# Last phase of a convolution, attention and experts kernel: W inverse evicted by two engines for two images, six of the last image's tile pairs added by VectorE

## The chip, the cores and the metric

The kernel runs on one core of a Trainium2 chip, in float32. A core has five engines that run side by side, each with its own queue of instructions in a fixed order: TensorE (PE; matmuls and transposes, into the PSUM memory; its weight loads are listed apart as PEld), VectorE (DVE), ScalarE (ACT), GpSimd (POOL) and SyncE (SP; here it issues DMA transfers). An instruction that needs another engine's result waits on a semaphore, and everything behind it in its queue waits too. PSUM is where TensorE writes; VectorE and ScalarE read it and "evict" results into the larger SBUF memory. The metric is the device time of one execution in microseconds (us), lower is better.

## The reference, cut to what matters

The input x is 32 images of 128 channels and 64 x 64 pixels.

```python
# layer 0: x + K-operator convolution of the group-normalized x
x_f = tensor_product(xc, _c(k11), _c(k12), False)        # butterflies along H and W
w_f = tensor_product(wc, _c(kd1), _c(kd2), False) * math.sqrt(H * W)
prod = jnp.einsum('bihw,oihw->bohw', x_f, w_f)
out = tensor_product(prod, _c(k21), _c(k22), True)       # inverse along H and W
x = x + jnp.real(out)
# layer 1, per image: 4096 tokens of 128 channels
t = t + _L1_attn_ref(_ln_t(t), Wk, bk, Wv, bv)           # scores over channels, softmax
t = t + _L1_ffn_ref(_ln_t(t), router_w, router_b, expert_w, expert_b)
# experts: softmax over 8, the best two, weights made to sum to 1
top_p, top_i = jax.lax.top_k(router_probs, K)
expert_out = jnp.einsum('bnd,edc->bnec', x, expert_w) + expert_b
return jnp.einsum('bnk,bnkc->bnc', top_p, gathered)
```

The second half of it, the inverse transforms, attention and experts, is the phase that is changed. The kernel computes all eight experts for every token and sums them with weights ("gates") of which six of eight are zero.

## The kernel before

It has three phases. The first (to about 974 us) normalizes and transforms the images and stores the result to HBM; the second (to about 2732 us) mixes channels at every frequency and stores the products, pf; the third works image by image on pf and x and writes the output. Only the third is changed.

**An image in the last phase.** Four builders add its steps to a plan.

- `transfers(b)`: SyncE loads eight tiles r0 to r7 of pf (ten buffers) and the image itself, y (two buffers).
- `conv(b)`: for each r tile e, `w_inverse` has TensorE make a PSUM tile pu of 128 x 1024 (eight matmuls, L818; step "w"), in the pool cv with ONE buffer of two banks; `w_out` copies it into the SBUF tile u by ScalarE (L828; steps "wo", two per tile, one for each half oh of pu's partitions, with two copies of 64 x 512 each, r = 0 and 1, which go to partitions 0 to 63 and 64 to 127 of u). When all eight are in u, `h_inverse` makes four PSUM tiles py, in the same pool cv (L840; "h"), and `h_out` adds each to y on VectorE (L848; "ho").
- `front(b)`: transposes of y into token tiles (pt, L899), their copies into tk on ScalarE ("to", L904), statistics on VectorE ("sa", L873; "va", L881 to L886), a power on GpSimd ("pwa", L891), "na" on VectorE (L928), normalized tokens xg on ScalarE (L939), the Gram matrix pg (L950), the chain of the softmax (gs, pa, rows, pb, t1, sm, pr, pc, prx: small steps that go back and forth between TensorE, VectorE and ScalarE), the product pp with the tokens (L1038), scaled by ScalarE (L1051, L1055) and added to tk by VectorE (L1066), a second power ("pwb"), and the router: logits, two maxima, an exponent on ScalarE ("f5", L1132), and the gates ("gt", L1137 to L1141, result oh).
- `experts(b)`: 32 tiles of 128 tokens. For a group of four: normalized tokens xn (ScalarE, L1166), transposed px (L1176), xT. For each token tile i and half (four experts): `expert` makes PSUM tile pe of 128 x 512 (L1189, three buffers); `gated` multiplies it by the gates into tm on VectorE (step "m", L1200). For each PAIR of token tiles (i // 2, 16 pairs an image) `summed` adds the eight products and the token tile tk on GpSimd (step "s", five instructions: two of L1211, one of L1212, two of L1214). tm holds a pair and has two buffers. `back` transposes four token tiles (po, L1221), `store` copies them (so, L1227) and SyncE writes them out.

**The order.** A builder gives each step an engine, an estimated time, a due time (in slots of 114 us per image, with a shift for each kind), what it comes after, and which buffers it takes and frees. `Plan.run` walks a model of the five engines with these estimates and writes down the order in which each engine's steps start: the earliest due among those that are ready. That is the order of each queue in the built program. The steps of three images are in flight at once: conv of image b beside front of b - 1 and experts of b - 2. In the built program the waits are set by a framework, from the data and the buffers that the instructions touch; the steps' own "after" lists only set the order.

```python
    plan = Plan({"cv": 1, "pe": 3, "tl": 3, "r": 10, "x": 2, "xg": NG, "xn": 2, "xT": 2, "tm": 2, "so": 2, "gate": 2})
    SLOT = 114.0
```

The first images have nothing beside them, so at the beginning conv(0) stands alone, and conv(1) is beside front(0); at the end the experts of image 31 stand alone.

Of the kernel before, what the change touches and what calls it, by code (L numbers as in the profile page):

```python
# [90 lines left out]
def kernel(  # L91
# [720 lines left out]
    def conv(b):  # L812
        def w_inverse(e):

            def run():
                ps = tile_of["cv", b, e] = cps.tile([P, 8, P], F32, tag="cv", name=f"pu{b}_{e}")
                for k in range(8):
                    nc.tensor.matmul(  # L818
                        ps[:, k, :], rs[b, e][:, k * P : (k + 1) * P], qw.rearrange("w r m -> w (r m)"),
                        start=True, stop=True,  # L820
                    )
            return run

        def w_out(e, oh):
            def run():
                ps = tile_of["cv", b, e]
                for r in range(2):
                    nc.scalar.copy(  # L828
                        u[r * n : (r + 1) * n, :, oh * n + 8 * e : oh * n + 8 * e + 8],
                        ps[oh * n : (oh + 1) * n, :, r * n : (r + 1) * n].rearrange("h o w -> h w o"),  # L830
                    )
            return run

        def h_inverse(g):
            def run():
                ps = tile_of["cy", b, g] = cps.tile([P, 16 * n], F32, tag="cv", name=f"py{b}_{g}")
                for k in range(16):
                    for oh in range(2):
                        rows = slice(oh * n, (oh + 1) * n)
                        nc.tensor.matmul(  # L840
                            ps[rows, k * n : (k + 1) * n], u[:, 16 * g + k, rows], hm, start=True, stop=True
                        )
            return run

        def h_out(g):
            def run():
                acc = xs[b][:, :, 16 * g : 16 * g + 16]
                nc.vector.tensor_tensor(  # L848
                    acc, tile_of.pop(("cy", b, g)).rearrange("o (w h) -> o h w", h=n), acc, ALU.add
                )  # L850
            return run

        for e in range(8):
            at = b + 0.08 * e
            add(b, f"w{e}", "PE", 1.8, at, w_inverse(e), [f"r{e}"] + [(b - 1, f"h{k}") for k in range(4)], ("cv",), ("r",))
            for oh in range(2):
                add(
                    b, f"wo{e}_{oh}", "ACT", 1.2, at, w_out(e, oh),
                    [f"w{e}"] + [(b - 1, f"h{k}") for k in range(4)], (), ("cv",) if oh else (),
                )  # L860
        for g in range(4):
            at = b + 0.68 + 0.07 * g
            add(b, f"h{g}", "PE", 2.15, at, h_inverse(g), [f"wo{e}_{oh}" for e in range(8) for oh in range(2)], ("cv",))
            add(b, f"ho{g}", "DVE", 1.25, at, h_out(g), [f"h{g}", "x"], (), ("cv",))
# [292 lines left out]
    def experts(b):  # L1157
        t = tk[b % 2]

        def normal(g):  # L1160
            def run():
                rstd, nmr = tile_of["norm", b]
                x = tile_of["xn", b, g] = wp.tile([P, 4, P], F32, tag="xn", name=f"xn{b}_{g}")
                for k in range(4):
                    i = 4 * g + k
                    nc.scalar.activation(  # L1166
                        x[:, k, :], t[:, i, :], AF.Identity, bias=nmr[:, i : i + 1], scale=rstd[:, i : i + 1]
                    )
            return run

        def turn(g):
            def run():
                x = tile_of.pop(("xn", b, g))
                ps = tile_of["px", b, g] = tps.tile([P, 512], F32, tag="tl", name=f"px{b}_{g}")
                for k in range(4):
                    nc.tensor.transpose(ps[:, k * P : (k + 1) * P], x[:, k, :], ident)  # L1176
            return run

        def turned(g):
            def run():  # L1180
                x = tile_of["xT", b, g] = wp.tile([P, 4, P], F32, tag="xT", name=f"xT{b}_{g}")
                nc.scalar.copy(x.rearrange("p k c -> p (k c)"), tile_of.pop(("px", b, g)))
            return run

        def expert(i, half):
            def run():
                es = slice(4 * half, 4 * half + 4)
                ps = tile_of["pe", b, i, half] = eps.tile([P, 512], F32, tag="pe", name=f"pe{b}_{i}_{half}")
                nc.tensor.matmul(  # L1189
                    ps, tile_of["xT", b, i // 4][:, i % 4, :], ew_sb[:, es, :].rearrange("d e c -> d (e c)"),  # L1190
                    start=True, stop=True,
                )
            return run

        def gated(i, half):
            def run():
                es = slice(4 * half, 4 * half + 4)
                if i % 2 == 0 and half == 0:
                    tile_of["tm", b, i // 2] = wp.tile([P, 2, NE, P], F32, tag="tm", name=f"tm{b}_{i}")
                nc.vector.tensor_tensor(  # L1200
                    tile_of["tm", b, i // 2][:, i % 2, es, :],
                    tile_of.pop(("pe", b, i, half)).rearrange("p (e c) -> p e c", c=P),
                    tile_of["gate", b][:, i, es].unsqueeze(2).to_broadcast([P, 4, P]), ALU.mult,
                )
            return run

        def summed(j):
            def run():
                tm, lo = tile_of.pop(("tm", b, j)), 2 * j
                for k in range(2):  # L1210
                    nc.gpsimd.tensor_tensor(tm[:, k, 0:4, :], tm[:, k, 0:4, :], tm[:, k, 4:8, :], ALU.add)  # L1211
                nc.gpsimd.tensor_tensor(tm[:, :, 0:2, :], tm[:, :, 0:2, :], tm[:, :, 2:4, :], ALU.add)  # L1212
                for m in range(2):
                    nc.gpsimd.tensor_tensor(t[:, lo : lo + 2, :], t[:, lo : lo + 2, :], tm[:, :, m, :], ALU.add)  # L1214
            return run

        def back(g):
            def run():
                ps = tile_of["po", b, g] = tps.tile([P, 512], F32, tag="tl", name=f"po{b}_{g}")
                for k in range(4):  # L1220
                    nc.tensor.transpose(ps[:, k * P : (k + 1) * P], t[:, 4 * g + k, :], ident)  # L1221
            return run

        def store(g):
            def run():
                so = wp.tile([P, 512], F32, tag="so", name=f"so{b}_{g}")
                nc.scalar.copy(so, tile_of.pop(("po", b, g)))  # L1227
                nc.sync.dma_start(ov[b][:, g * 512 : (g + 1) * 512], so)
            return run

        s2 = b + 2
        for g in range(8):
            at = s2 + 0.125 * g
            add(b, f"xn{g}", "ACT", 1.7, at - 0.1, normal(g), ["nb"], ("xn",))
            add(b, f"px{g}", "PE", 0.55, at - 0.05, turn(g), [f"xn{g}"], ("tl", "xT"), ("xn",))
            add(b, f"xT{g}", "ACT", 0.6, at - 0.05, turned(g), [f"px{g}"], (), ("tl",))
            for k in range(4):
                i = 4 * g + k
                for half in range(2):
                    add(  # L1240
                        b, f"pe{i}_{half}", "PE", 0.86, at + 0.125 * (2 * k + half) / 8, expert(i, half), [f"xT{g}"],
                        ("pe",), ("xT",) if k == 3 and half else (),
                    )
                    add(
                        b, f"m{i}_{half}", "DVE", 0.7, at + 0.125 * (2 * k + half) / 8, gated(i, half),
                        [f"pe{i}_{half}", "gt"] + ([f"m{i - k % 2}_0"] if k % 2 or half else []), ("tm",) if k % 2 == 0 and half == 0 else (),
                        ("pe",) + (("gate",) if i == NT - 1 and half else ()),
                    )
                if k % 2:
                    add(  # L1250
                        b, f"s{i // 2}", "POOL", 5.45, at + 0.125 * (2 * k + 2) / 8, summed(i // 2),
                        [f"m{i - 1 + a}_{h}" for a in range(2) for h in range(2)], (), ("tm",),
                    )
            add(b, f"st{g}", "PE", 0.55, at + 0.25, back(g), [f"s{2 * g}", f"s{2 * g + 1}"], ("tl",))
            add(b, f"so{g}", "ACT", 0.6, at + 0.25, store(g), [f"st{g}"], (), ("tl",))
# [61 lines left out]
```

## Time and profile before

| | us |
|---|---|
| median of five runs (lowest, highest) | 6379.27 (6372.46, 6384.12) |
| the profiled execution | 6376.22 |
| its span, first to last instruction | 6374.5 |
| TensorE busy | 6118.0 (96%) |
| VectorE busy | 4196.8 (66%) |
| ScalarE busy | 3759.9 (59%) |
| GpSimd busy | 4204.5 (66%) |
| experts' matmuls, L1189 (4096 instructions) | 1985.7 |
| gated products, L1200 (2048) | 1353.0, 0.684 each |
| W inverse copies, L828 (1024) | 594.1, 0.580 each |
| GpSimd sums, L1211, L1212, L1214 | 1308.2, 652.8, 760.0 |

The profile comes from one execution. In its groups a row gives line, engine, operation, output <- input, shapes and count, then the busy time in us and the mean of one in ns, then the idle time of that engine before them and what ended it. In a timeline a row gives start and length in us, engine, line and operation, how many instructions were merged, and in brackets the idle time before and its releaser. A float32 matmul or transpose counts as two instructions on TensorE. The span in 40 slices, TensorE's busy tenths, the clock granted to it, and GpSimd:

```
PE   7999999999999999969999999999999999999987
POOL 2110005666666666506888888888888888888889
PEclk9999999999999999989999999999999999999999
```

The last phase begins in slice 18.

### The profile page before, as it was taken

What the parts mean: (1) busy time and instruction counts of PE and PEld (TensorE: products, weight loads), DVE (VectorE), ACT (ScalarE), POOL (GpSimd) and SP (SyncE); (2) the same over time, 40 slices, a digit from 0 to 9 for tenths busy, and PEclk for the clock granted to TensorE, in tenths of its full rate; (3) what the DMA queues carried; (4) which work ended last, traced back from release to release, by engine and by line L of the source; (5) the groups of instructions that cost most, each with busy time, mean ns of one, the idle gap of its engine ahead of it and who ended that gap; (6) DMA issues with size and microseconds to landing.
All of it is one profiled execution on the core that took longest, in us unless ns stands there. A gap on an engine that the chain in (4) does not pass through costs nothing. (4 is left out here: it accounts for less than half of the span.)

```text
span 6374.5 us, 218347 instructions
## 1 busy us (share of the span) xinstructions
PE 6118.0 (96%) x94922; PEld 4789.6 (75%) x94922; DVE 4196.8 (66%) x7626; ACT 3759.9 (59%) x7089; POOL 4204.5 (66%) x3780
## 2 busy tenths in 40 slices
PE   7999999999999999969999999999999999999987
PEld 7899998999999999966666666666666666666653
DVE  5555544555555555527787878777787878787776
ACT  6666663444444444446666667666667666666752
POOL 2110005666666666506888888888888888888889
PEclk9999999999999999989999999999999999999999
DMA  5666656666666666552121212222222212121100
GB/s 202 217 208 226 221 204 173 159 157 162 159 158 158 156 157 158 134 141 93 63 96 62 95 62 93 67 85 73 83 77 70 88 63 95 61 96 62 67 19 25
DMA packets 556965, 756.55 MB, mean 119 GB/s; under 512 B 58466, under 2 KB 321892, under 8 KB 551908
## 3 DMA queue, kind: packets, MB, share of 16 engines
q1 hardware_dynamic: 554096, 741.38, 38.4%
q8 instruction: 745, 12.21, 0.8%
q14 instruction: 216, 1.77, 0.1%
q10 hardware_dynamic: 1908, 1.19, 0.1%
HBM read 406.80 MB, written 335.54 MB: 116 GB/s over the span
## 5 line engine op out<-in xcount | busy, mean ns | idle before, releaser
L1189 PE MATMUL pe<-ew_sb,xT 128*128 128x512 f32 x4096 | 1985.7, 602 | 51.0 <-DVE tm L1200 50.7
L1200 DVE TENSOR_TENSOR tm<-pe,oh 128x512 f32<-128x512 f32 x2048 | 1353.0, 684 | 564.3 <-PE pe L1189 421.8
L1211 POOL TENSOR_TENSOR tm<-tm 128x512 f32<-128x512 f32 x1024 | 1308.2, 1293 | 307.8 <-DVE tm L1200 256.0
L1189 PEld LDWEIGHTS pe<-ew_sb,xT 128*128 128x128 f32 x4096 | 691.4, 191 | 523.7 <-issue 332.0
L623 PE MATMUL m<-f,s 128*64 128x64 f32 x32768 | 1068.7, 224 | 5.8 <-POOL s L574 4.4
L623 PEld LDWEIGHTS m<-f,s 128*64 128x64 f32 x32768 | 998.3, 138 | 67.4 <-POOL s L574 4.7
L574 POOL COPY s<-l 128x512 f32<-128x512 f32 x512 | 548.2, 1105 | 734.5 <-issue 654.4
L612 ACT COPY f<-g 128x1024 f32<-128x1024 f32 x512 | 518.7, 1013 | 671.1 <-PE g L601 644.2
L612 DVE COPY f<-g 128x1024 f32<-128x1024 f32 x512 | 627.0, 1225 | 348.0 <-PE g L601 340.1
L1214 POOL TENSOR_TENSOR tk<-tk,tm 128x256 f32<-128x256 f32 x1024 | 760.0, 742 | 80.3
L828 ACT COPY u<-pu 64x512 f32<-64x512 f32 x1024 | 594.1, 580 | 306.4 <-PE pu L818 295.4
L601 PE MATMUL g<-c,wst 9*128 9x128 f32 x16384 | 726.2, 287 | 25.7 <-ACT f L612 3.5
L1212 POOL TENSOR_TENSOR tm<-tm 128x512 f32<-128x512 f32 x512 | 652.8, 1275 | 40.1
L601 PEld LDWEIGHTS g<-c,wst 9*128 9x128 f32 x16384 | 579.8, 186 | 109.9 <-DVE f L612 69.4
L818 PEld LDWEIGHTS pu<-qw,r 128*128 128x128 f32 x4096 | 501.9, 196 | 169.4 <-ACT u L828 92.1
L633 DVE COPY o<-m 64x1024 f32<-64x1024 f32 x256 | 314.0, 1227 | 469.0 <-ACT o L633 421.5
L818 PE MATMUL pu<-qw,r 128*128 128x128 f32 x4096 | 520.8, 282 | 62.8 <-ACT u L828 52.9
L345 POOL TENSOR_TENSOR grstd<-gms,mhalf 128x1 f32<-128x1 f32 x32 | 17.7, 554 | 784.4 <-DVE gms L341 755.2
L414 PE MATMUL pf<-ph,v 128*128 128x128 f32 x4096 | 495.6, 279 | 19.3 <-issue 12.8
L576 POOL TENSOR_SCALAR s<-l 128x512 f32<-128x512 f32 x256 | 503.7, 1968 | 0.0
L414 PEld LDWEIGHTS pf<-ph,v 128*128 128x128 f32 x4096 | 470.2, 193 | 30.9 <-issue 14.4
L1227 ACT COPY so<-po 128x512 f32<-128x512 f32 x256 | 150.9, 590 | 574.4 <-issue 412.2
(165 smaller groups left out, 8617.6 us busy)
## 6 DMA issues: line engine op xcount, KB each, us to landing
xf<-f SPq DMA_DIRECT2D x512, 256.0 KB, 3.9
l<-xf SPq DMA_DIRECT2D x1024, 128.0 KB, 3.2
pf<-o SPq DMA_DIRECT2D x1024, 128.0 KB, 2.4
r<-pf SPq DMA_DIRECT2D x512, 256.0 KB, 4.7
x<-in_x_dram SPq DMA_DIRECT2D x256, 256.0 KB, 5.4
y<-in_x_dram SPq DMA_DIRECT2D x32, 2048.0 KB, 8.2
out_dram<-so SPq DMA_DIRECT2D x256, 256.0 KB, 2.0
tw<-in_tw_dram SPq DMA_DIRECT2D x6, 384.0 KB, 6.1
```

The lines of the kernel that those rows point to most:

```text
L414: nc.tensor.matmul(pl[:, j * P : (j + 1) * P], vs[b][:, 8 * g + j, :], ph.rearrange("h r m -> h (r m)"), start=True, stop=True,)
L574: nc.gpsimd.tensor_copy(dst, src)
L601: nc.tensor.matmul(pg[g // 2][:, g % 2, m * P : (m + 1) * P], wst[rows, 16 * half + 4 * t + m, :], c[rows].rearrange("r h k -> r (h k)"), ...
L612: copy(f.rearrange("i m (g o) -> i m g o", g=2), tile_of["g", w, half, t][k].rearrange("i g (o m) -> i m g o", o=4))
L623: nc.tensor.matmul(ps[hh * n : (hh + 1) * n, q, :], s[:, h].rearrange("i k b -> i (k b)")[:, B * r : B * r + n], f[:, h, r, :], start=(r = ...
L818: nc.tensor.matmul(ps[:, k, :], rs[b, e][:, k * P : (k + 1) * P], qw.rearrange("w r m -> w (r m)"), start=True, stop=True,)
L828: nc.scalar.copy(u[r * n : (r + 1) * n, :, oh * n + 8 * e : oh * n + 8 * e + 8], ps[oh * n : (oh + 1) * n, :, r * n : (r + 1) * n].rearran ...
L1189: nc.tensor.matmul(ps, tile_of["xT", b, i // 4][:, i % 4, :], ew_sb[:, es, :].rearrange("d e c -> d (e c)"), start=True, stop=True,)
L1200: nc.vector.tensor_tensor(tile_of["tm", b, i // 2][:, i % 2, es, :], tile_of.pop(("pe", b, i, half)).rearrange("p (e c) -> p e c", c=P), t ...
L1211: nc.gpsimd.tensor_tensor(tm[:, k, 0:4, :], tm[:, k, 0:4, :], tm[:, k, 4:8, :], ALU.add)
L1212: nc.gpsimd.tensor_tensor(tm[:, :, 0:2, :], tm[:, :, 0:2, :], tm[:, :, 2:4, :], ALU.add)
L1214: nc.gpsimd.tensor_tensor(t[:, lo : lo + 2, :], t[:, lo : lo + 2, :], tm[:, :, m, :], ALU.add)
```

## The change

Three edits, all in the last phase:

1. In `conv`, for the images 0 and 1 (`shared`), `w_out` is split by r in place of oh: the first step of a tile (ScalarE) copies both halves oh for r = 0, the second (now VectorE, estimated at 1.4 us) both halves for r = 1. For these two images "w" of tile e also stands after the first step of tile e - 1. From image 2 on the copies are those of before.
2. In `experts`, for the last image (31), the pairs 2, 5, 8, 10, 13 and 15 (`direct`) get `weighed` in place of `gated`: four scalar_tensor_tensor on VectorE for each half, each of which multiplies the 128 columns of one expert in pe by its gate and adds the token tile in tk, in place (estimated at 1.2 us for the four). These pairs have no tm and no step on GpSimd.
3. `back` of a group follows the products themselves where a pair has no sum.

Since the order is made anew by `Plan.run` from these steps, the queues of the images 0 to 4 and 31 change in places that the diff doesn't show; the rest keeps its order.

```diff
-        def w_out(e, oh):
+        shared = b < 2
+
+        def w_out(e, k):
             def run():
                 ps = tile_of["cv", b, e]
-                for r in range(2):
-                    nc.scalar.copy(
+                for j in range(2):
+                    r, oh = (k, j) if shared else (j, k)
+                    copy = nc.vector.tensor_copy if shared and k else nc.scalar.copy
+                    copy(
                         u[r * n : (r + 1) * n, :, oh * n + 8 * e : oh * n + 8 * e + 8],
                         ps[oh * n : (oh + 1) * n, :, r * n : (r + 1) * n].rearrange("h o w -> h w o"),
                     )
...
-            add(b, f"w{e}", "PE", 1.8, at, w_inverse(e), [f"r{e}"] + [(b - 1, f"h{k}") for k in range(4)], ("cv",), ("r",))
+            add(b, f"w{e}", "PE", 1.8, at, w_inverse(e), [f"r{e}"] + ([f"wo{e - 1}_0"] if shared and e else []) + [(b - 1, f"h{k}") for k in range(4)], ("cv",), ("r",))
             for oh in range(2):
                 add(
-                    b, f"wo{e}_{oh}", "ACT", 1.2, at, w_out(e, oh),
+                    b, f"wo{e}_{oh}", *(("DVE", 1.4) if shared and oh else ("ACT", 1.2)), at, w_out(e, oh),
...
+        def weighed(i, half):
+
+            def run():
+                ps = tile_of.pop(("pe", b, i, half))
+                for e in range(4):
+                    nc.vector.scalar_tensor_tensor(
+                        t[:, i, :], ps[:, e * P : (e + 1) * P], tile_of["gate", b][:, i, 4 * half + e : 4 * half + e + 1],
+                        t[:, i, :], ALU.mult, ALU.add,
+                    )
+            return run
+
+
+        direct = (2, 5, 8, 10, 13, 15) if b == B - 1 else ()
...
                     add(
-                        b, f"m{i}_{half}", "DVE", 0.7, at + 0.125 * (2 * k + half) / 8, gated(i, half),
-                        [f"pe{i}_{half}", "gt"] + ([f"m{i - k % 2}_0"] if k % 2 or half else []), ("tm",) if k % 2 == 0 and half == 0 else (),
+                        b, f"m{i}_{half}", "DVE", 1.2 if i // 2 in direct else 0.7, at + 0.125 * (2 * k + half) / 8,
+                        weighed(i, half) if i // 2 in direct else gated(i, half),
+                        [f"pe{i}_{half}", "gt"] + ([f"m{i - k % 2}_0"] if k % 2 or half else []),
+                        ("tm",) if k % 2 == 0 and half == 0 and i // 2 not in direct else (),
...
-                if k % 2:
+                if k % 2 and i // 2 in direct:
+                    made[b, f"s{i // 2}"] = made[b, f"m{i}_1"]
+                elif k % 2:
                     add(
                         b, f"s{i // 2}", "POOL", 5.45, at + 0.125 * (2 * k + 2) / 8, summed(i // 2),
```

## The prediction, made before the changed kernel ran

> **What bounds the kernel now.** I read the slices of the span first, then the two ends of the last phase (it starts at 2736): the chain of waits, waits by stretch, the timeline, the groups by form. The order of the new instructions and what each waits for are read from the built program. In the middle TensorE has no room; this row of the stretch table gives its busy time in 3000 us:
>
> ```profile
> 3200.00:6200.00 3000.00, 2950.92 (x20430) 1983.47 (x20431) 2345.65 (x5198) 1972.43 (x4551) 2626.84 (x2254) 1.00 0.22 74
> ```
>
> TensorE is first, 98.4%. An image costs 113 us of TensorE work, so what the first images lose in TensorE idle time is not won back, and a gain there would stay. The end is another matter. The chain of waits, followed to the last instruction (start, length, what):
>
> ```profile
> 6359.45 2.45 POOL tm L1211 x2
> 6361.99 1.26 POOL tm L1212
> 6363.32 0.74 POOL tk L1214
> 6364.12 0.72 POOL tk L1214
> 6364.84 2.44 POOL tm L1211 x2
> ...
> 6370.28 0.70 PE po L1221 x2
> 6371.05 0.59 ACT so L1227
> ```
>
> From 6283.3 on GpSimd adds up one pair of token tiles after the other, each 5.41 us from start to start (6364.84 less 6359.45 is 5.39), 16 pairs to 6370.2. VectorE waits for it, because the products' two buffers are full (waits from 6282 to 6370: us, times, longest):
>
> ```profile
> DVE tm L1200 <- POOL tk L1214: 33.7, 13, 2.8
> ```
>
> The beginning (timeline of the first image's W inverse; waits of 2735 to 2804):
>
> ```profile
> 2757.53 3.57 PE L818 MATMUL pu<-qw,r 128*128 128x128 f32 x16 [2.48 <-ACT u L828]
> ...
> 2761.14 2.39 ACT L828 COPY u<-pu 64x512 f32<-64x512 f32 x4 [3.66 <-PE pu L818]
> ...
> 2763.58 3.28 PE L818 MATMUL pu<-qw,r 128*128 128x128 f32 x16 [2.48 <-ACT u L828]
> ```
> ```profile
> PE pu L818 <- ACT u L828: 14.8, 6, 2.5
> ```
>
> There is one buffer for pu, so TensorE (2.05 to 3.6 us a tile, the clock granted varies) and ScalarE's four copies (2.39) take turns.
>
> **The tail.** Six of 16 pairs leave GpSimd: 6 x 5.41 = 32.5 us off its chain, which becomes 10 x 5.41 = 54.1. It would end near 6338 if nothing else were slower. Each such pair loses 4 products of 0.65 to 0.69 on VectorE (L1200) and gets 16 scalar_tensor_tensor of 128x128, PSUM and tk in, tk out, the gate as a scalar by partition. In the built order each waits for the one before (same rows of tk). No row shows this form. The nearest, by shape:
>
> ```profile
> L1066 DVE TENSOR_TENSOR tk<-pp,tk 128x384 f32<-128x384 f32 x320 | 175.5, 548 | 42.6 <-ACT lq L1055 42.1
> ...
> L1124 DVE SCALAR_TENSOR_TENSOR lg<-oh,lg 128x256 f32<-128x256 f32 x32 | 16.8, 524 | 0.0
> ...
> L1066 DVE TENSOR_TENSOR tk<-pp,tk 128x256 f32<-128x256 f32 x32 | 13.2, 414 | 0.0
> ...
> L764 DVE SCALAR_TENSOR_TENSOR ebb<-ebb,pm 128x512 f32<-128x512 f32 x2 | 1.4, 688 | 21.9 <-PE pm L763 21.9
> ```
>
> L1066 has the same operands: 134 ns less for 128 columns less, so 0.28 at 128. L764 against L1200 (688, 684) says that this operation costs no more than a product. A dependent instruction follows 0.04 after the end (L1066 from 2855.95 for 0.56, its bn_stats at 2856.55). So 0.32 each, 16 x 0.32 = 5.1 a pair. Below: eight bn_stats of 128 columns in 1.65, 0.20 each. Above: L1124, slowed beside GpSimd, 0.52, less 0.13 for half the columns, plus 0.04: 0.43. I take 0.32, as L1066 stays at 0.55 (maximum 0.56) beside a GpSimd that is 88% busy.
>
> Now the new pace. Pairs 0 and 1 run as before, 6281.9 to 6290.6 (TensorE restarts slowly there). The direct pairs take 6 x 5.1 = 30.7. Between them stand two gated pairs three times, and one twice. TensorE needs 8 x 0.86 and two blocks of transposes at 0.44 for two gated pairs, 7.8, and has about 0.8 of it done, three pe buffers deep, when the direct pair ends: 7.0. For one pair it is 3.9 less 0.8, 3.1. Together 8.7 + 30.7 + 3 x 7.0 + 2 x 3.1 = 66.6, and the last addition ends at 6348.5. GpSimd's last sum (pair 14) gets its last product near 6343.5 and ends near 6348, just ahead. What follows (transposes, copy, store) stays 4.3 us. Gain 6370.2 - 6348.5 = 21.7. At 0.20 TensorE and GpSimd hold the end near 6345: 25. From 0.32 on, every 0.01 costs 0.96, so at 0.43 the gain is 11.
>
> **The start.** The diff gives ScalarE the copies with r = 0 and VectorE those with r = 1. Both read both halves oh of the same pu. In the built order VectorE's first copy waits for ScalarE's second copy of the same tile: the engines take turns. The old trace has such a pair on one PSUM tile in the mixing phase:
>
> ```profile
> 2694.79 1.01 ACT L633 COPY o<-m 64x1024 f32<-64x1024 f32 x1 [1.19 <-PE m L623]
> ...
> 2695.83 1.23 DVE L633 COPY o<-m 64x1024 f32<-64x1024 f32 x1 [1.83 <-ACT o L633]
> ```
>
> VectorE starts 0.03 after ScalarE's end (2695.80), and 421.5 us of its waits in the whole span are of this kind.
>
> The Trainium skill ("PSUM — Partial Sum Buffer", PSUM bank collisions) has a rule that speaks against this edit: two engines must not touch one bank in one group of 32 partitions at a time, two reads included, though other groups of the bank are free. By it the two halves oh, on partitions 0 to 63 and 64 to 127, could be read side by side, the split by r can't; side by side a tile would take some 1.3 us instead of 2.4. L633 reads other partitions with each engine and is still in turn, so the row doesn't show the rule's free case.
>
> So a tile costs ScalarE 1.19, handover 0.03, VectorE two copies (TENSOR_TENSOR x2 of 512 columns: 1.27; I take 1.29), and 0.09 around: 2.60 instead of 2.48. Seven such gaps in image 0: +0.9.
>
> Image 1's W inverse lies beside image 0's front, and here the new order matters. VectorE's queue now holds u copies ahead of "va" (L881 to L886), and "na" behind the copies of tile 5. Before, from the first pt (2803.70): va at 13.0, xg at 25.6, first pp at 48.8. After, tile by tile: pt and tiles 0, 1 to 10.2; tiles 2 to 5 each 2.05 + 2.6 = 4.65, so tile 3 ends at 19.6, va to 20.5, GpSimd's power (5.46) to 26.1, tile 5 and na 29.2; xg (12.4 on ScalarE) 29.3 to 41.7, then the copies of tile 6 and tile 7 (TensorE 2.05) to 47.6. The four py of image 1 now stand between pa, pb and pc: py 2.05 and ho 1.23 four times with the chain of softmax between, first pp at 60.0. That is 11.2 later, with 4 x 2.03 = 8.1 of py already done: net +3.1.
>
> From there ScalarE sets the pace: 11 groups of pp at 1.49 (15.9) and six copies of 0.59 put the last at 80.3 against 69.8; the second power ends at 89.4 against 77.4. The exponent of the gates (L1132) stands in ScalarE's queue behind seven tiles of image 2 rather than five, so the gates come at 108.5 against 96.5. TensorE reaches image 2's first py at 112.4 against 107.3, with four pe (0.86) and one px (0.44) fewer behind it, 3.9: a lag of 9.0 in TensorE's work (the 3.1 is part of it). After that it is full in both. With 0.9 for image 0 and 1 for a lower clock in the longer waits the start costs 10.9. Bounds: 3, if TensorE wins back all that it still waits from 2900 to 3326 (3.9, 1.1, 1.2 and 1.3 us in the waits of four stretches); 17, if four or five more tiles take 3.4 instead of 2.05 (as at 2757). Loads and stores keep their number and, but for the six tiles' stores coming sooner, their order on SP's queue; the r tiles of image 0 are all issued by 2760, ahead of their use in both.
>
> **Sum.** -21.7 + 10.9 = -10.8: span 6374.5 to 6363.7, that execution 6376.22 to 6365.4. The median of the five runs is 6379.27, 3 above it, so 6368.5 for a median. 0.2% is 12.8 us, about what a measurement of this kernel can tell from no change.
>
> **Rivals.**
> - The start's lag is absorbed (TensorE waits less at later places as the gates catch up): start 0 to 5, 6358 to 6363. For it: ScalarE has 34% idle in the middle. Against: TensorE has 1.6%.
> - The start lags more: low clock and gates later still, 22: 6379.6, no change. For it: 0.84 granted in 2820 to 2850 already.
> - The additions contend with GpSimd, and the kernel is slower. Two-operand work from SBUF does: L1119 takes 0.42 alone and 1.38 in the median. If tk or the gate's scalar brings that, by L885's 0.70 beside 0.18, each takes 0.32 + 0.5; 96 x 0.5 = 48 us on VectorE in the tail, the gain turns to 21.7 - 48 = -26, with the start +37: 6416. It decides from 0.43, where the two ends cancel, and the kernel is slower by over 0.2% from 0.57. Against: L1066.
> - The edit does at the start what its words say, two evictions at once: 8 tiles x 1.1 and a quicker front, about -8 more: -30, 6349. Against: the wait in the built order.
>
> **How the numbers follow.** Forecast 0.60, over 6363 to 6375 (0.16 of it below 6366.5); absorbed 0.19; more lag 0.09; contention 0.07; parallel 0.05. Faster 0.16 + 0.19 + 0.05 = 0.40, same 0.44 + 0.09 = 0.53, slower 0.07. The range 6356 to 6380 leaves out contention, the parallel case and a little of the rest.
>
> **What would show it.** VectorE's u copies each idle until ScalarE's; the gates of image 0 some 108 us after its first pt instead of 96; TensorE's busy time of the first 170 us of the phase spread over 11 us more; the new additions near 0.28 long and 0.32 apart; GpSimd idle in the tail; the last adder VectorE, near 66 us after the last gates. Wrong if u copies overlap, if the middle starts no later than before, or if an addition takes 0.4.

## The result, and the profile after

The changed kernel takes 6396.97 us (median of 41 runs, 6383.73 to 6408.59); the kernel before, run beside it, takes 6384.12 (77 runs, 6371.90 to 6399.13). The ratio is 1.0019, with a 95% interval of 1.0015 to 1.0023: about 12 us slower. The forecast was 6368.5 and its range ended at 6380.

The profiled execution after has a span of 6399.2 us, 24.7 more than the one before. Not all of that is the change: its first pu tile starts at 2743.26 instead of 2736.38, before anything that was changed.

Because lines were added, pu is still L818, its copies are now L833, py L845, pt L904, pp L1043, the exponent L1137, the gated products L1205 and the new additions L1217.

**The start.** Three views answer to those of before. First the timeline of image 0's W inverse:

```profile
2768.84 1.19 ACT L833 COPY u<-pu 64x512 f32<-64x512 f32 x2 [5.44 <-PE pu L818]
2770.06 1.41 DVE L833 COPY u<-pu 64x512 f32<-64x512 f32 x2 [5.22 <-ACT u L833]
...
2771.86 3.75 PE L818 MATMUL pu<-qw,r 128*128 128x128 f32 x16 [3.05 <-issue]
2775.65 1.19 ACT L833 COPY u<-pu 64x512 f32<-64x512 f32 x2 [5.62 <-PE pu L818]
2776.87 1.41 DVE L833 COPY u<-pu 64x512 f32<-64x512 f32 x2 [5.40 <-ACT u L833]
```

VectorE starts 0.03 us after ScalarE's end (2768.84 plus 1.19 is 2770.03), and TensorE after VectorE's end: the two engines take turns. TensorE's gap between tiles is 2.85 to 3.05 us where it was 2.44 to 2.48. And no full tile of image 0 takes 2.05 us any more; after the gaps they take 3.40 to 3.76 us, where two of six took 2.05 before. The waits from 2743 to 2820 (us in total, times, longest) say the same:

```profile
DVE u L833 <- ACT u L833: 40.7, 8, 9.7
```

Then the softmax chain of image 0, in TensorE's timeline (idle time and releaser in brackets):

```profile
2870.22 0.38 PE L972 MATMUL pa<-ident,gs 128*1 128x128 f32 x2
...
2873.07 3.49 PE L845 MATMUL py<-hm,u 128*64 128x64 f32 x64 [1.95 <-DVE u L833]
2876.50 0.59 PE L983 MATMUL pb<-wv_sb,gs 128*128 128x128 f32 x2
...
2877.88 2.08 PE L845 MATMUL py<-hm,u 128*64 128x64 f32 x64 [0.38 <-DVE y L853]
...
2881.29 2.09 PE L845 MATMUL py<-hm,u 128*64 128x64 f32 x64 [0.49 <-DVE y L853]
2883.31 0.33 PE L1016 MATMUL pc<-ident,pr 128*128 128x128 f32 x1
...
2884.71 2.08 PE L845 MATMUL py<-hm,u 128*64 128x64 f32 x64 [0.94 <-DVE y L853]
2886.72 2.47 PE L1043 MATMUL pp<-prx,y 128*128 128x144 f32 x18
```

The four py of image 1 now stand between the short steps pa, pb, pc and the first pp. From pa to pp takes 16.5 us; before it took 9.9 (2842.62 to 2852.48), with the last two pu tiles of image 1 inside it and the py behind. Last, the end of image 0's router (timeline of ScalarE and VectorE):

```profile
2927.61 0.18 DVE L1133 TENSOR_TENSOR tops<-tops 128x32 f32<-128x32 f32 x1
...
2935.20 1.17 ACT L833 COPY u<-pu 64x512 f32<-64x512 f32 x2 [0.47 <-PE pu L818]
2936.40 0.23 ACT L1137 ACTIVATE tops<-tops 128x32 f32<-128x32 f32 x1
...
2936.66 0.18 DVE L1142 TENSOR_SCALAR tops<-tops 128x32 f32<-128x32 f32 x1 [8.87 <-ACT tops L1137]
```

The exponent's input is ready at 2927.8 (107.7 us after the first pt, 2820.09), but in ScalarE's queue the exponent stands behind copies of image 2's pu tiles and starts at 2936.40, 8.6 us later; VectorE idles 8.87 us. That wait is not new. Before:

```profile
2889.29 0.18 DVE L1128 TENSOR_TENSOR tops<-tops 128x32 f32<-128x32 f32 x1
...
2897.40 0.24 ACT L1132 ACTIVATE tops<-tops 128x32 f32<-128x32 f32 x1
...
2897.55 0.87 DVE L873 BATCH_NORM_STATS2 bs<-tk 128x6 f32<-128x128 f32 x4 [8.07 <-ACT tk L904]
```

There the input is ready at 2889.47 (85.8 us after the first pt, 2803.70) and the exponent starts 7.9 us later. VectorE idles 8.07 us too, put down to a copy of ScalarE's that comes just ahead of the exponent. Image 0's gated products start 118.4 us after its first pt, 96.5 before; in both that is 10.7 us after the exponent's input is ready. So the 21.9 us arise ahead of the exponent.

What this costs is read as one stretch, from image 0's first pt to the last image's first gated product (us, TensorE busy with its records, clock, DMA share, GB/s). Before:

```profile
2803.70:6281.89 3478.19, 3392.26 (x23530) 0.99 0.22 74
```

After:

```profile
2820.09:6322.28 3502.19, 3403.73 (x23530) 0.99 0.22 73
```

TensorE does the same 23530 instructions and takes 24.0 us longer: 11.5 us more busy time, which is longer matmuls, and 12.5 us more idle time (98.5 against 85.9). The granted clock of the first 46.3, the next 50 and the next 50 us was 0.82, 0.86 and 0.93, where before it was 0.88, 0.90 and 1.00.

**The tail.** The chain that ended last (start, length, what) ends on VectorE's additions, no longer on GpSimd:

```profile
6394.53 0.36 DVE tk L1217
6394.91 0.36 DVE tk L1217
...
6395.73 0.59 ACT so L1246
```

VectorE's timeline near the end, and the new group by its form:

```profile
6379.90 6.15 DVE L1217 SCALAR_TENSOR_TENSOR tk<-pe,oh,tk 128x128 f32<-128x128 f32 x16 [0.24 <-PE pe L1194]
6385.97 2.05 DVE L1205 TENSOR_TENSOR tm<-pe,oh 128x512 f32<-128x512 f32 x3
```
```profile
L1217 DVE SCALAR_TENSOR_TENSOR tk<-pe,oh,tk 128x128 f32<-128x128 f32 x96 | 33.1, 350 | 5.1 <-PE pe L1194 1.4
```

An addition takes 0.350 us by its own record (0.36 with what follows in the chain), and they come 0.385 apart, 6.15 for a pair. From the last image's first gated product to the end of the span are 76.9 us; before, 92.6 (6374.5 less 6281.89; a timeline counts from the span's start). So the tail gained 15.7 and the start lost more.

### The profile page after: what moved, and what is told of

Its sections match the earlier page's. It is cut to its first block, busy times and chain, and to the rows that moved or that the text cites. A ratio compares the mean times of both kernels' runs of the same rounds, so it can differ in the third digit from the quotient of the medians.

```text
span 6399.2 us, 218438 instructions
## 1 busy us (share of the span) xinstructions
PE 6136.7 (96%) x94922; PEld 4802.5 (75%) x94922; DVE 4240.5 (66%) x7730; ACT 3741.2 (58%) x7057; POOL 4174.0 (65%) x3750
## 3 DMA queue, kind: packets, MB, share of 16 engines
q10 hardware_dynamic: 1908, 1.19, 0.1%
## 5 line engine op out<-in xcount | busy, mean ns | idle before, releaser
L1205 DVE TENSOR_TENSOR tm<-pe,oh 128x512 f32<-128x512 f32 x2024 | 1339.3, 684 | 532.9 <-PE pe L1194 428.1
L1230 POOL TENSOR_TENSOR tm<-tm 128x512 f32<-128x512 f32 x1012 | 1293.1, 1292 | 316.1 <-DVE tm L1205 262.8
L833 ACT COPY u<-pu 64x512 f32<-64x512 f32 x992 | 575.5, 580 | 330.6 <-PE pu L818 320.2
L1231 POOL TENSOR_TENSOR tm<-tm 128x512 f32<-128x512 f32 x506 | 645.4, 1276 | 39.7
L818 PEld LDWEIGHTS pu<-qw,r 128*128 128x128 f32 x4096 | 509.5, 199 | 174.2 <-issue 97.5
L818 PE MATMUL pu<-qw,r 128*128 128x128 f32 x4096 | 528.8, 284 | 68.4 <-issue 33.0
L345 POOL TENSOR_TENSOR grstd<-gms,mhalf 128x1 f32<-128x1 f32 x32 | 17.7, 554 | 792.0 <-DVE gms L341 763.1
L414 PEld LDWEIGHTS pf<-ph,v 128*128 128x128 f32 x4096 | 470.4, 193 | 33.5 <-issue 15.8
```

Source lines behind the costliest of these rows:

```text
L414: nc.tensor.matmul(pl[:, j * P : (j + 1) * P], vs[b][:, 8 * g + j, :], ph.rearrange("h r m -> h (r m)"), start=True, stop=True,)
L818: nc.tensor.matmul(ps[:, k, :], rs[b, e][:, k * P : (k + 1) * P], qw.rearrange("w r m -> w (r m)"), start=True, stop=True,)
L833: copy(u[r * n : (r + 1) * n, :, oh * n + 8 * e : oh * n + 8 * e + 8], ps[oh * n : (oh + 1) * n, :, r * n : (r + 1) * n].rearrange("h o w ...
L1205: nc.vector.tensor_tensor(tile_of["tm", b, i // 2][:, i % 2, es, :], tile_of.pop(("pe", b, i, half)).rearrange("p (e c) -> p e c", c=P), t ...
```

## The experiments

All were timed against the kernel before on the same chip. A difference in us is the ratio less one, times the median of before in those runs (6388.4, 6388.0 or 6385.6).

**Each part alone.** e1 keeps the last image's edit, e2 the first two images', e3 and e4 split e2 by image.

```diff
# e1
-        shared = b < 2
+        shared = False
# e2
-        direct = (2, 5, 8, 10, 13, 15) if b == B - 1 else ()
+        direct = ()
# e3: e2 and            # e4: e2 and
+        shared = b < 1  # +        shared = b == 1
```

> Only the last image's edit: images 0 and 1 are evicted as before. Theory (read from the profile after: tail from the last image's first gated product to the end 76.9 us instead of 92.6): -15.7 us against the kernel before, about 6368 at a median of 6384 for before. Rival 1 (the forecast's own tail): -21.7, 6362. Rival 2 (the tail gains nothing by itself, and the chain just ends on another engine): 6384.

Measured: 0.9976 (0.9965 to 0.9986), -15.3 us. In its profile the tail takes 77.1 us.

> Only the first two images' edit: no pair is added by VectorE. Theory (the whole difference of the medians, +12.9, plus the tail's 15.7): +28.5 us, about 6412.5. Rival 1 (the forecast's own start): +10.9, 6395. Rival 2 (the profiled execution's +33.5 holds in all executions): 6417.5.

Measured: 1.0039 (1.0027 to 1.0052), +24.9.

> Only image 0's W inverse is evicted by two engines; image 1 and the tail as before. Theory: the gap of 2.9 us instead of 2.48 keeps TensorE at the lower clock, all seven tiles take 3.4 to 3.75 us, first transposes 9.5 us later than in before, and nothing of it comes back: +9.5, about 6393.5. Rival: the front of image 0 absorbs most of it: 6384 to 6387.

Measured: 1.0008 (0.9999 to 1.0017), +5.1, which the interval doesn't tell from nothing nor from the 9.5. The profiles say why 9.5 was too much: from image 0's first pu to its first pt are 76.3 to 76.8 us in the three profiles with the shared copies (after, e2, e3), and 66.9 to 75.1, mean 70.5, in nine with ScalarE's copies (before, e1, e4 to e7, e9 to e11). The profile of before, with 67.3, is at the low end of the nine.

> Only image 1's W inverse is evicted by two engines; image 0 and the tail as before. Theory: the loss that the profile after shows behind the first transposes (33.5 less 9.5 in that execution, 28.5 less 9.5 by the medians) belongs to image 1: +19 to +24, 6403 to 6408, with image 0's gates some 20 us later after its first transposes than in before. Rival: most of it is image 0's (a late start and a cold clock carried on): 6384 to 6390.

Measured: 1.0035 (1.0022 to 1.0048), +22.4; gates at 117.1. Image 1's part is most of the loss. The parts add up: -15.3 + 5.1 + 22.4 = 12.2, where the whole change measures 1.0019, 12.1.

**Order or hand-over?** In image 1 the edit does two things: VectorE takes half the copies, in turn, and the plan, which takes the two for parallel, puts all queues in another order. e5 has the new order without VectorE, e6 VectorE without the new order.

```diff
# e5: e4 and
-                    copy = nc.vector.tensor_copy if shared and k else nc.scalar.copy
+                    copy = nc.scalar.copy
# e6: e4 and
-            add(b, f"w{e}", ..., [f"r{e}"] + ([f"wo{e - 1}_0"] if shared and e else []) + ...
+            add(b, f"w{e}", ..., [f"r{e}"] + ...
-                    b, f"wo{e}_{oh}", *(("DVE", 1.4) if shared and oh else ("ACT", 1.2)), at, w_out(e, oh),
+                    b, f"wo{e}_{oh}", "ACT", 1.2, at, w_out(e, oh),
```

> Image 1 only, tail as before: every queue in the order that the two-engine plan made (e4), but all four copies of a tile by ScalarE. Theory O (the order is the loss: py of image 1 ahead of pp, the gates' exponent behind more tiles): most of e4's +22 stays, +13 to +18 against before. Rival C (the hand-over and VectorE's slower copies, with the clock that they cost, are the loss): +0 to +6.

Measured: 1.0030 (1.0019 to 1.0042), +19.2; first pp at 66.2, gates at 118.0.

> Image 1 only, tail as before: TensorE's and ScalarE's order as in the kernel before, but the copies with r = 1 by VectorE, right behind ScalarE's. Theory O: +0 to +6 against before. Rival C: +13 to +18. If both e5 and e6 lose some 10, order and hand-over each have a share.

Measured: 1.0008 (0.9998 to 1.0017), +5.1; first pp at 51.1, gates at 97.4. Theory O holds: the order is the loss, whoever copies. The turns themselves cost nothing that can be told from zero there.

**Is it the clock?** e7 fills TensorE's gap behind four tiles.

```diff
# e7: e4 and, behind the eight matmuls of w_inverse
+                if b == 1 and 2 <= e <= 5:
+                    warm = eps.tile([P, 512], F32, tag="pe", name=f"warm{e}")
+                    for k in range(8):
+                        nc.tensor.matmul(warm[:, 0:P], qw..., qw..., start=True, stop=True)
```

> e4 (image 1 only) with eight more matmuls behind tiles 2 to 5 of image 1's W inverse, on qw alone and into a PSUM tile that nobody reads, in the gap in which TensorE waits for the copies. Theory: the gap of 2.9 us is what brings the low clock; with 0.9 us of it left, tiles 3 to 6 take 2.05 instead of 3.0 to 3.75 us, so 5 us less than e4: +16 to +18 against before. Rival (the low clock comes from something else, or the chain doesn't hang on these tiles): as e4, +22, or worse by the matmuls' own time.

Measured: 1.0023 (1.0014 to 1.0032), +14.7. Tiles 3 to 6 take 2.02 us each (3.65, 3.47, 3.07 and 3.75 in e4), so filling the gap takes the slow tiles away: the granted clock from 12 to 38 us after the first pt is 0.94, where it is 0.70 in e4. But the interval (8.9 to 20.4 us) overlaps e4's (14.1 to 30.7), and in the profiles the stretch from first pt to the last image's first product is only 1.5 us shorter than e4's. What those four tiles lose is a part of the loss at most.

**Which displaced step?** Three orders are put back one at a time in e4.

```diff
# e9: py of image 1 behind the softmax chain of image 0
-            ..., [f"wo{e}_{oh}" for e in range(8) for oh in range(2)], ("cv",))
+            ..., [f"wo{e}_{oh}" for e in range(8) for oh in range(2)] + ([(0, "prx")] if b == 1 else []), ("cv",))
# e10 and e11, in the "after" list of the copies
+ ([(0, "f5")] if b == 2 and e >= 5 else [])    # e10: exponent first
+ ([(0, "na")] if b == 1 and e >= 5 else [])    # e11: xg first
```

> e4 (image 1 only, +22 against before), with the four py of image 1 planned behind the softmax chain of image 0: first pp some 10 us behind the last pg, as in before, instead of 19. The exponent of the gates then stands behind five of image 2's tiles again, as in before. Theory: these two are most of the loss; first pp 56 to 58 us after the first pt, gates near 105: +5 to +10 against before. Rival (TensorE's work has to be done anyway, so its order costs nothing): +18 to +24.

Measured: 1.0021 (1.0012 to 1.0029), +13.4; first pp at 59.1, gates at 106.9. Its TensorE timeline at the same place:

```profile
2866.54 0.38 PE L972 MATMUL pa<-ident,gs 128*1 128x128 f32 x2
...
2870.61 0.49 PE L992 MATMUL pb<-t,wk_sb 128*128 128x128 f32 x2 [0.38 <-DVE t L988]
...
2873.20 0.47 PE L1016 MATMUL pc<-ident,pr 128*128 128x128 f32 x1 [1.69 <-ACT pr L1012]
...
2874.30 4.42 PE L1043 MATMUL pp<-prx,y 128*128 128x144 f32 x18 [0.39 <-DVE prx L1020]
2878.65 2.09 PE L845 MATMUL py<-hm,u 128*64 128x64 f32 x64
```

From pa to pp are 7.8 us instead of 16.5, though TensorE waits in between where it had worked on py. The py then fit between the pp, where ScalarE sets the pace.

> e4, with the gates' exponent of image 0 planned ahead of the copies of image 2's tile 5 on ScalarE; py and pp as in e4. Theory: VectorE's 8.9 us of waiting for the exponent goes, gates near 110 us after the first pt, and 6 to 9 us of e4's loss: +13 to +16. Rival (the gates wait for nothing that counts): +20 to +24.

Measured: 1.0028 (1.0018 to 1.0039), +17.9; gates at 112.4. VectorE's idle time for the exponent falls to 2.7 us. Since before has the wait as well, this takes away something that the change had not brought in.

> e4, with image 1's tile 5 copied behind the normalized tokens xg of image 0, as in before, and with it one py and a half fewer ahead of pp. Theory: xg starts 5 to 6 us sooner and all of the chain with it; first pp near 61, +13 to +16. Rival (xg isn't what the chain hangs on): +20 to +24.

Measured: 1.0023 (1.0014 to 1.0032), +14.7; first pp at 63.4, gates at 110.3.

By their times none of the three lies surely below e4, whose interval is 14.1 to 30.7 us; e9, with 7.7 to 18.5, comes nearest to it. The profiles tell them apart better, since the stretch from image 0's first pt to the last image's first product leaves out what image 0's copies and the second phase vary by (us; idle is the stretch less TensorE's busy time; the last three columns count from image 0's first pt or are against before):

| | stretch | busy, against before | idle, against before | first pp | gates |
|---|---|---|---|---|---|
| before | 3478.2 | 3392.3 | 85.9 | 48.8 | 96.5 |
| e1, e3 | +1.6, +1.0 | +2.0, +1.6 | -0.4, -0.6 | 50.0, 47.0 | 97.7, 94.2 |
| after | +24.0 | +11.5 | +12.5 | 66.6 | 118.4 |
| e4 image 1 only | +22.0 | +9.4 | +12.6 | 66.9 | 117.1 |
| e5 new order, ScalarE | +26.2 | +10.4 | +15.8 | 66.2 | 118.0 |
| e6 old order, two engines | +4.9 | -0.3 | +5.2 | 51.1 | 97.4 |
| e7 gap filled | +20.5 | +12.6 | +7.9 | 63.3 | 113.5 |
| e9 py late | +8.6 | +3.5 | +5.0 | 59.1 | 106.9 |
| e10 exponent first | +17.7 | +8.2 | +9.5 | 66.6 | 112.4 |
| e11 xg first | +17.5 | +3.2 | +14.3 | 63.4 | 110.3 |
| e8, e12 (below) | +4.4, +3.0 | +1.6, +0.7 | +2.8, +2.3 | 47.6, 48.9 | 94.8, 96.6 |

(e7's busy time holds 64 more instructions, some 8 us.) Image 1 is as before in e1, e3, e8 and e12, which ought to be 0 and are 1.0 to 4.4, so one profile doesn't tell some 4 us from nothing. Against e4's 22.0, e9 wins back 13.4, clear of that; e10's 4.3 and e11's 4.5 are at its edge, and so is e6's +4.9. That the three add up to 22 shows nothing, since e10 takes out a wait that before has too. In e9 the exponent stands behind five tiles again and still starts 7.9 us after its input, as in before, so the 13.4 are those of the py and what follows from them. The low clock goes with the order: e5, without VectorE, has as much more busy time as e4, and e6 has none.

**Two engines that don't take turns.** e8 gives image 0's tiles 2 to 7 two PSUM tiles of one bank each, in the pool of pe, which is idle then; ScalarE copies one while VectorE copies the other. Image 1 is as before, the tail as changed.

```diff
# e8: e1 and
+        apart = range(2, 8) if b == 0 else ()
...
+        def w_half(e, k):
...
+                ps = tile_of["cw", b, e, k] = eps.tile([P, 512], F32, tag="pe", name=f"pv{b}_{e}_{k}")
+                for o in range(4):
+                    nc.tensor.matmul(ps[:, o * P : (o + 1) * P], rs[b, e][:, (4 * k + o) * P : (4 * k + o + 1) * P], ...
...
+                add(b, f"w{e}_{k}", "PE", 1.0, at, w_half(e, k), ..., ("pe",), ("r",) if k else ())
+                add(b, f"wo{e}_{k}", "DVE" if k else "ACT", 1.6, at, half_out(e, k), [f"w{e}_{k}"], (), ("pe",))
```

> The tail as changed, image 1 as before. Image 0's tiles 2 to 7 are made as two PSUM tiles of one bank each in the experts' pool (three buffers, idle then), and ScalarE copies the one while VectorE copies the other. Theory: the turns are what makes two engines useless; apart, a tile costs TensorE's 2.05 us and no gap, image 0's first transposes come 50 to 57 us after its first pu instead of 67 to 76, and with the tail's -15: -32 to -40 against before. Rival (copies of two engines slow each other, or the loads of r are next): -15 to -22.

Measured: 0.9938 (0.9924 to 0.9951), -39.6 us, 6350.5. The first pt comes 48.1 us after the first pu. Its timeline:

```profile
2760.91 1.50 ACT L845 COPY u<-pv 64x256 f32<-64x256 f32 x4 [13.59 <-PE pv L832]
2761.87 1.76 DVE L845 COPY u<-pv 64x256 f32<-64x256 f32 x4 [1.09 <-PE pv L832]
...
2764.28 9.25 PE L832 MATMUL pv<-qw,r 128*128 128x128 f32 x72
```

VectorE's copies start while ScalarE's run (2760.91 to 2762.41), and TensorE makes 72 instructions, four tiles and a half, in one go of 9.25 us: 2.06 a tile, without a gap and without a slow one.

e8 changes two things at once: two engines copy side by side, and TensorE has three buffers in place of one, so that it seldom waits for a copy. No run has the buffers with ScalarE alone. An estimate from the rows: ScalarE's four copies of a half take 1.50, so 3.0 for a tile; before, the six tiles took 5.41 each (2757.53 to the first py at 2789.99), in e8 2.06 where TensorE doesn't wait. The buffers by themselves could then save 2.4 of 3.35 us a tile, the larger part of e8's gain.

**The tail, woven.** e12 is e8 with the additions of a pair's two token tiles taken in turn, so that most do not need the one just before; TensorE makes a pair's pe tiles in that order too.

```diff
# e12: e8 and
...
+                for a, half, e in tiles:      # in turn: two token tiles i and i + 1
+                    ps, k = tile_of["pe", b, i + a, half], 4 * half + e
+                    nc.vector.scalar_tensor_tensor(
+                        t[:, i + a, :], ps[:, e * P : (e + 1) * P], tile_of["gate", b][:, i + a, k : k + 1],
+                        t[:, i + a, :], ALU.mult, ALU.add,
+                    )
```

> e8 (image 0's tiles 2 to 7 in separate banks, and the tail), with the additions of two token tiles of a pair taken in turn, so that most don't wait for the one before. Theory: they come 0.27 to 0.30 us apart instead of 0.385, the tail is 7 to 10 us shorter than 77.1, and the whole -45 to -50 against before. Rival (an addition's own 0.35 us is what sets the pace, or TensorE's three buffers): -36 to -41.

Measured: 0.9929 (0.9917 to 0.9941), -45.3 us, 6337.63: the lowest median here, below both kernels. Its interval (-53.0 to -37.7) overlaps e8's (-48.5 to -31.3), so the gain of the weave itself is read from the profiles: the tail takes 71.1 us instead of 77.1. Its VectorE timeline:

```profile
6285.71 4.73 DVE L1259 SCALAR_TENSOR_TENSOR tk<-pe,oh,tk 128x128 f32<-128x128 f32 x16
...
6290.35 2.05 DVE L1234 TENSOR_TENSOR tm<-pe,oh 128x512 f32<-128x512 f32 x3
```

Sixteen additions in 4.73 us instead of 6.15: 0.29 apart in the mean (4.73 less the last one's 0.34, by 15), though each lasts 0.34. Four of the 15 still need the one just before and start 0.38 to 0.39 after it; the other eleven start after 0.26 to 0.27. The six pairs gain less than 6 x 1.42 = 8.5, because VectorE now waits for TensorE's pe in places.

## Why the prediction was wrong

**The turns: right.** VectorE's copies idled until ScalarE's, with 0.03 between. The pair of copies was taken at 1.29 and took 1.39 to 1.41, and TensorE began 0.21 to 0.39 after VectorE's end, where it had begun 0.05 after ScalarE's and 0.09 was allowed for the whole tile. So the gap is 2.85 to 3.05 instead of 2.60.

**Image 0, +0.9: too small.** Measured +5.1 (-0.6 to 10.9), which alone doesn't exclude 0.9; between the means of the profiles it is 6.0, and their ranges don't overlap. The term counted seven longer gaps and no slower tile; the longer gap has none of the fast tiles that the shorter one still has now and then.

**Image 1, "a lag of 9.0 in TensorE's work" with "1 for a lower clock": the step that failed.** The mechanism was there: va and xg later, py between pa, pb and pc. Its sizes were not. va ran from 22.0 to 22.9 (foreseen 19.6 to 20.5), xg began at 34.5 (29.3), the first pp came at 66.6 (60.0), the gates at 118.4 (108.5), image 2's first py at 123.8 (112.4). First, tiles 3 to 6 were counted at 2.05 us and took 2.97 to 3.75. Tiles 3, 4 and 5 alone (3.65, 3.42 and 2.97) are 3.9 us over, and "na", which stands behind the copies of tile 5, ran 0.03 us after them; with the longer gaps this makes up about the 5.2 us by which xg came late, and in e7, where the gap is filled, xg began at 31.1. Second, from the end of the second power to the exponent's input passed 11.5 us, where the prediction kept the 8.4 of before. The exponent itself cost next to nothing against before: it stood behind six and a half tiles, not seven, and waited 8.6 us against 7.9. Third, the term "1 for a lower clock in the longer waits" was 11.5 by the busy time, with the idle time at 12.5: about as much was lost in slow matmuls as in waiting, and a count of TensorE's lag at full speed sees only the waiting. The prediction put slow tiles into its upper bound of 17, as "four or five more tiles"; the whole start measures 24.9 (17.2 to 33.2) in e2. Nor is it the hand-over that lags: the new order costs +19.2 without VectorE's copies (e5). How the 11.5 us spread over the displaced steps stays open.

**The tail, -21.7: right in form, one duration mis-sized.** GpSimd idles, VectorE adds last, the direct pairs set the pace. The addition was taken at 0.28 long and 0.32 apart, by the row of L1066; it is 0.350 and 0.385. By the prediction's own rule (0.96 us for each 0.01 from 0.32 on) that takes 6.2 off: 15.5, and e1 measures 15.3 (8.9 to 22.4).

**The rivals.** "The start lags more" was the true one, with the price at 22 (24.9 in e2); with the shorter gain of the tail it ends above before instead of at 6379.6. "The start's lag is absorbed" fell: 24 us were still there 3400 us later. Contention of the additions did not show: 0.340 to 0.353 us in all 96. "Evictions parallel after all" fell by the turns; e8, where copies do run side by side, is 24.3 below e1, with more buffers as well.

**Sum.** The forecast's -21.7 + 10.9 became -15.3 + 27.5 (5.1 and 22.4). Of the 28.5 us between 6368.5 and 6396.97, 6 are the tail's, 17 the start's, and 5 lie in the median of the kernel before, 6384.12 with 77 runs in place of 6379.27 with five.

## What to carry to other kernels

An order made by a planner from estimated times follows the estimates: telling it that two engines share a job moved the chain of small, dependent steps behind large independent ones, and that cost some 19 us, where the shared copies by themselves cost 5 or nothing. Before giving a copy to a second engine, ask whether the built program lets the two touch the tile at once. Separate tiles in separate banks did, and with their three buffers they were worth some 24 us; how much of it the buffers alone would bring was not run. An idle stretch in the profile after is a loss only if the same place in the profile before lacks it; the wait for the exponent was in both. Price waits of TensorE with the slow matmuls that follow, and look at several executions before taking one duration for the rule.

## What was not expected of the hardware

After gaps of 2.85 to 3.05 us in the W inverse of images 0 and 1 (after, e2, e3, e4, e6, e9, e10, e11), TensorE's next tile took 2.65 to 3.76 us in all 44 cases, never 2.05. After gaps of 2.44 to 2.54 us it took 2.05 in 11 of 73 and up to 3.78 in the others, and this differs from execution to execution of the same code. With the gap filled by matmuls that nobody reads (e7), all four took 2.02. The gap just before is not the whole of it: image 1's last tile took 3.03 us after a gap of 0.52 in before, and 3.65 after 0.93 in e6. The Trainium skill ("TensorE: Matmul & The Clock Gate", the section on why this matters for your kernels) asks for no idle gaps over some 3 us between bursts; here tiles behind gaps below that already ran slow.

An addition on VectorE that needs the result of the one just before it starts 0.38 to 0.39 us after that one's start, one that doesn't 0.26 to 0.27 (e12; in after the step from one token tile to the next, the only one inside a pair that needs no result, is 0.27). The Trainium skill ("VectorE: DVE Perf Modes", the section on the DRAIN you can't avoid) reports eight copies that take the same time with and without a semaphore after each; for these additions the runs show 0.12 us for each such wait.
